# A two-layer graph network on one Trainium2 core: attention matrix and logit row transposed by block loads and VectorE, norm statistics on ScalarE, another order of rounds

## The chip, the cores and the metric

The kernel runs on one core of one Trainium2 chip. A core has TensorE (PE, matrix products; PEld is its weight load), VectorE (DVE), ScalarE (ACT), GpSimd (POOL), and SyncE (SP), whose queue here issues nearly all transfers; 16 DMA engines carry them. The metric is the device time in microseconds of one execution. Before the change the median of three runs is 2782.28 us (2780.95 to 2782.86).

## The reference

There are 64 batches of 256 tokens with 512 features, all in float32, and one 256 x 256 adjacency matrix `adj` of zeros and ones. Two layers follow each other, each with a residual and a norm over the features:

```
# layer 0: masked attention, 8 heads of 64
q, k, v = x @ Wq + bq, x @ Wk + bk, x @ Wv + bv
scores  = q k^T / 8 + (1 - adj) * -1e9
x       = layernorm(x + softmax(scores) v @ Wo + bo)

# layer 1: additive attention
h   = x @ W;   s1 = h . a1;   s2 = h . a2
e   = leaky_relu(s1[i] + s2[j], 0.2) * adj
att = softmax(e)
x   = layernorm(x + elu(att @ h + beta * h))
```

## The kernel before, in words

The batches are taken two at a time ("pairs", 32 of them). Within a pair the stages are named after what TensorE does. `x`: the pair's input is brought in transposed (features on partitions) as `xT`. `q`, `k`, `v`: three projections of both batches together. Then, for each batch `s` of the pair (0 or 1): `scores` (keys by queries, for 8 heads), `sums` (denominators by products with ones), `mix` (attention times v), `o` (output projection, added to the batch's `X`), a norm, `logits` (the row of s2 on all partitions), `attention` (the second attention matrix, transposed), `spread` (X^T times that matrix, giving `yT`), and `u` (the product with `W`). After `u` comes `finish`: elu, residual, norm and the store. The products of `q`, `k`, `v`, `o`, `spread` and `u` are done by seven instead of eight block products (`project`, from line 414); the block sums that this needs are made by POOL (`token_sums` and the sums around line 963). The weights of q and k stream in as seven pieces per pair through six buffers ("piece").

For the second attention, two VectorE products with accumulation (L877) give s1 and s2 per token. TensorE transposes the s2 column, broadcast to 128 columns, into a row on all partitions in PSUM (`pe_row`, L887). VectorE adds s1 (`z`, L896), applies the leaky relu (`e`, L902), POOL multiplies by the mask (L905), VectorE takes the maximum (L907), ScalarE exponentiates with sums (L910), VectorE divides and adds beta to the diagonal (L913, L916). TensorE then transposes the four 128 x 128 blocks of `e` into PSUM (`pe_att`, L923) and ScalarE copies them out as `attT` (L927). Batch 63 ("last") takes a path of its own.

A norm of 128 tokens (`norm`, L553) is bn_stats and bn_aggr on VectorE (L556, L557), the reciprocal root on POOL (L560, L561), minus mean times root on VectorE (L564), and one ScalarE pass over the 512 features with that scale and bias (L566).

The input `xT` is loaded in blocks of 32 x 32 elements (L588: four transfers per batch, one for every group of 32 partitions, pieces of 128 bytes) so that one VectorE instruction, which transposes within blocks of 32 x 32, completes the transpose (L591).

What sets the order: every operation is first recorded with an engine, an estimated cost in ns and its dependences (`Plan.op`). TensorE's order is written by hand: `ROUND` is the cyclic order of stages, and `LATER` says how many rounds after the pair's own number each stage comes. An operation's `claims` name buffers that it takes into use. `Plan.place` then plays the schedule through with the estimated costs, with `LAG` as the time from an operation's end to its effect on another engine (2200 ns for SP), and with the number of buffers in `slots`; the order found is the order in which each engine's instructions are emitted. Each engine, SP's queue among them, then works in that order, and each waits where its next instruction is not ready. The last 60 TensorE operations are free of the written order. A TensorE operation of cost 0 emits nothing; it only fixes from which place of the order its buffers may be claimed.

Of the kernel before, what the change touches and what calls it, by code (L numbers as in the profile page):

```python
# [16 lines left out]
P = 128  # L17
# [4 lines left out]

ROUND = ("sums1", "mix1", "scores0", "v", "o1", "attention0", "u1", "x", "spread0", "sums0", "mix0", "scores1", "q",
         "logits1", "o0", "u0", "attention1", "k", "spread1", "logits0")

LATER = {"x": -2, "q": -1, "k": -1, "v": 0, "scores0": 0, "scores1": 0, "sums0": 0, "sums1": 1, "mix0": 0, "mix1": 1,
         "o0": 0, "o1": 1, "logits0": 0, "logits1": 1, "attention0": 1, "attention1": 1, "spread0": 1, "spread1": 1,
         "u0": 1, "u1": 2}
# [25 lines left out]
class Plan:  # L54
# [9 lines left out]

    LAG = {"PE": 260.0, "DVE": 70.0, "ACT": 70.0, "POOL": 90.0, "SP": 2200.0}
    SWITCH = 250.0
# [161 lines left out]
def gnn_two_layers(ctx: ExitStack, tc: tile.TileContext, x, adj, Wq, bq, Wk, bk, Wv, bv, Wo, bo, W, a, beta, out):  # L228
# [12 lines left out]

    slots = {"xin": 2, "x": 4, "two": 6, "xP": 1, "piece": 6, "full": 4, "half": 18, "xS": 2, "st": 80, "ps": 8, "rows": 4}

# [14 lines left out]
    def sb(tag, shape, name):  # L258
        return Buf(sb_pool, tag, [P] + shape, name)
# [4 lines left out]
    def st(n, name):  # L264
        return sb("st", [n], name)
# [286 lines left out]

    def norm(X, t):  # L553

        bn, mv, rs, nm = st(6, "bn"), st(2, "mv"), st(1, "rs"), st(1, "nmr")
        plan.op("DVE", 690, lambda: nc.vector.bn_stats(bn[A], X[:, t, :]), [(X, (t, 0)), (X, (t, 1))], [bn])  # L556
        plan.op("DVE", 175, lambda: nc.vector.bn_aggr(mv[A], bn[A]), [bn], [mv])  # L557

        def rsqrt():
            nc.gpsimd.tensor_scalar(rs[A], mv[:, 1:2], EPS, None, ALU.add)  # L560
            nc.gpsimd.tensor_tensor(rs[A], rs[A], neg_half, ALU.pow)  # L561

        plan.op("POOL", 800, rsqrt, [mv], [rs])
        plan.op("DVE", 150, lambda: nc.vector.scalar_tensor_tensor(  # L564
            nm[A], mv[:, 0:1], -1.0, rs[A], op0=ALU.mult, op1=ALU.mult), [mv, rs], [nm], mode="two")
        plan.op("ACT", 810, lambda: nc.scalar.activation(  # L566
            X[:, t, :], X[:, t, :], AF.Identity, bias=nm[A], scale=rs[A]),
            [nm, rs], [(X, (t, 0)), (X, (t, 1))])

    def pair(m, at, general=False):  # L570

        def turn(what):

            plan.turn = ((m or 0) + LATER[what], ROUND.index(what))

# [5 lines left out]
        V = sb("two", [2 * NT, D], f"v_{m}")  # L581

        def blocks(s):

            xb = sb("xin", [C, N], f"xin_{m}_{s}")
            rows = x[at].rearrange("o (b j) (c f i) -> o f j c b i", j=32, f=4, i=32)[s]
            for f in range(4):
                plan.op("SP", 700, lambda f=f: nc.sync.dma_start(  # L588
                    xb[f * 32:(f + 1) * 32].rearrange("p c (b i) -> p c b i", i=32), rows[f]), [], [(xb, f)],
                    first=m == 0 and s == 0 and f == 0)  # L590
            plan.op("DVE", 1140, lambda: nc.vector.transpose(  # L591
                xT[A].rearrange("p c (t s n) -> p c t s n", t=NT, s=2)[:, :, :, s, :],
                xb[A].rearrange("p c (t n) -> p c t n", t=NT)), [xb, (xT, "turn")], [(xT, (t, s)) for t in range(NT)])


        turn("x")
        plan.op("PE", 0, lambda: None, [], [(xT, "turn")], claims=[xT])
        for s in range(2):
            blocks(s)

# [33 lines left out]
    def batch(m, s, qT, kT, V, dram, general):  # L634
# [10 lines left out]

        def finish(t, us, u, mode):

            m = sb("half", [D], "m")
            plan.op("ACT", 640, lambda: nc.scalar.activation(m[A], u(), AF.Exp), us, [m])
            plan.op("DVE", 700, lambda: nc.vector.scalar_tensor_tensor(  # L650
                X[:, t, :], u(), 0.0, X[:, t, :], op0=ALU.max, op1=ALU.add), us, tokens(t), mode=mode)
            plan.op("DVE", 700, lambda: nc.vector.scalar_tensor_tensor(
                X[:, t, :], m[A], 1.0, X[:, t, :], op0=ALU.min, op1=ALU.add), [m], tokens(t), mode="two")
            norm(X, t)
            plan.op("SP", 1400, lambda: nc.sync.dma_start(
                dram(out, s)[:, t, :], X[:, t, :]), tokens(t), [])

# [34 lines left out]
        def attention_by_keys():  # L692
# [30 lines left out]
            def denominators():  # L723
                turn("sums")

                acc = ps([N], "ps_den")

                def pe():
                    for i in range(2):
                        for c in range(C):  # L730
                            nc.tensor.matmul(acc[32 * c:32 * c + 32, :], ones[:, 16 - 16 * i:48 - 16 * i],  # L731
                                             both[c][:, i, :], start=i == 0, stop=i == 1)

                plan.op("PE", 1000, pe, both, [acc], mode="sums", claims=[inv])
                plan.op("DVE", 1750, lambda: nc.vector.reciprocal(inv[A], acc[A]), [acc], [inv])
                for i, d in enumerate((acc, inv)):
                    junk = sb("half", [N], "junk")
                    plan.op("ACT", 600, lambda i=i, d=d, junk=junk: nc.scalar.activation(
                        junk[A], d[A], AF.Identity, accum_out=range_sb[:, i, b:b + 1]), [d],
                        [junk, (range_sb, (i, b))])  # L740
                if last:
                    select = sb("half", [H, HD], "select")
                    plan.op("DVE", 690, lambda: nc.vector.tensor_copy(
                        select[A], ident[:, 0:P:P // H].unsqueeze(2).to_broadcast([P, H, HD])), [acc], [select])
                    return [spread_last(select, inv, g) for g in range(2)]
                plan.op("SP", 60, lambda: nc.sync.dma_start(rows[A], inv[0:P:P // H, :]), [inv], [rows])
                for i in range(2):
                    def spread(i=i):
                        r = rows[A]
                        nc.sync.dma_start(everywhere[i * HD:(i + 1) * HD], bass.AP(  # L750
                            tensor=r.tensor, offset=r.offset + i * N, ap=[[0, HD], [2 * N, C], [1, N]]))

                    plan.op("SP", 1500, spread, [rows], [(everywhere, i)])

# [107 lines left out]
        else:  # L862
# [3 lines left out]
            project(left["o"], right_o, False, [], onto, onto)  # L866
        for t in range(NT):
            norm(X, t)
        if b == 0:
            plan.turn = (0, ROUND.index("k"))  # L870
            left["w"] = second_layer_constants()

        sv = [st(2, "s") for t in range(NT)]
        for t in range(NT):
            for i in range(2):
                junk = sb("half", [D], "junk")
                plan.op("DVE", 780, lambda t=t, i=i, junk=junk: nc.vector.scalar_tensor_tensor(  # L877
                    junk[A], X[:, t, :], 1.0, wa_sb[:, i, :], op0=ALU.mult, op1=ALU.mult,
                    accum_out=sv[t][:, i:i + 1]), tokens(t) + [(wa_sb, i)], [junk, (sv[t], i)],
                    mode="two")  # L880


        row = ps([N], "tr_s")

        def pe_row():
            for t in range(NT):
                nc.tensor.transpose(row[:, blk(t)], sv[t][:, 1:2].to_broadcast([P, P]), ident)  # L887

        z, e = sb("half", [NT, N], "z"), sb("half", [NT, N], "e")
        turn("logits")  # L890
        plan.op("PE", 220, pe_row, sv, [row], claims=[z, e])
        nm1, sm1, rc1 = st(NT, "nm1"), st(NT, "sm1"), st(NT, "rc1")
        tra = ps([NT, N], "tr_a")
        attT = sb("half", [NT, N], "attT")
        for t in range(NT):
            plan.op("DVE", 480, lambda t=t: nc.vector.tensor_scalar(  # L896
                z[:, t, :], row[A], sv[t][:, 0:1], None, ALU.add), [row, sv[t]], [(z, t)])

        for ts in ((0, 1), (1, 2)) if last else ((0, 2),):
# [19 lines left out]

            def pe_att(ts=ts):  # L920
                for j in range(NT):
                    for t in range(NT)[ts]:
                        nc.tensor.transpose(tra[:, j, blk(t)], e[:, t, blk(j)], ident)  # L923

            turn("attention")
            plan.op("PE", 215 * k, pe_att, part, [(tra, t) for t in range(NT)[ts]], claims=[attT])
        plan.op("ACT", 590, lambda: nc.scalar.copy(attT[A], tra[A]), [tra], [(attT, i) for i in range(4)])  # L927

        yT = sb("full", [C, N], f"yT_{b}")
        if last:  # L930
# [20 lines left out]
            for t in range(NT):  # L951
                finish(t, [us[t]], lambda t=t: us[t][A], None)
            return
# [37 lines left out]

        for t in range(NT):
            finish(t, [(u, (t, 0)), (u, (t, 1))], lambda t=t: u[:, t, :], "two")

# [65 lines left out]
```

## Time and profile before

| | |
|---|---|
| median of three runs | 2782.28 us |
| the profiled execution | 2782.27 us |
| its span, first to last instruction | 2780.4 us |
| mean granted TensorE clock | 0.995 |
| ACT COPY attT<-tr_a (L927) | 64 times, 586 ns each |
| DVE BATCH_NORM_STATS2 (L556) | 256 times, 681 ns each |
| DVE oT<-oT,inv_all (L776) | 126 times, 894 ns each |
| SP's queue, longest kind of wait (L588 behind DVE yT L478) | 28 times, 832.2 us in all |
| DMA, mean over the span | 94 GB/s; queue q1 34.0% of 16 engines |
| DMA packets | 429313, of them 279448 under 512 B |

How to read it: busy time is the time in which an engine ran at least one instruction. In a group of instructions, the columns are line, engine, operation, out<-in, shapes, count, then busy microseconds and mean ns of one, then the idle time just before them and what ended it. In the chain and in the timeline the columns are start and length in microseconds and what ran. Engines run side by side, and matmuls of TensorE overlap each other in it, so busy times and durations do not add up to the span.

### The profile page before, as it was taken

The numbers are of one execution on the slowest core, as the hardware profiler recorded it, in microseconds if no ns is written. First come the engines' busy times: TensorE is split into PE (matmuls) and PEld (weight loads), VectorE is DVE, ScalarE is ACT, GpSimd is POOL, SyncE is SP. The second block draws the span as 40 slices with busy tenths as digits, with TensorE's granted clock in tenths as the row PEclk, the third lists the DMA queues.
The fourth block names the chain that finished last, engine by engine and source line by source line (L and its number), as shares of the span: only waits on it lengthen the run. The fifth ranks groups of instructions, "written<-read, shape, count | busy, mean of one in ns | idle before, by whom it ended". The sixth has DMA issues, their size and how long they took to land.

```text
span 2780.4 us, 46736 instructions
## 1 busy us (share of the span) xinstructions
PE 2738.3 (98%) x16259; PEld 2312.2 (83%) x16259; DVE 2067.6 (74%) x4190; ACT 1238.7 (45%) x2747; POOL 1759.1 (63%) x2379
## 2 busy tenths in 40 slices
PE   7999999999999999999999999999999999999997
PEld 6788888888888888888888888888888888888875
DVE  6777777787776777777877767777778777677777
ACT  2344444454454444444544544444445445444443
POOL 5666666666666666666666666666666666666664
PEclk9999999999999999999999999999999999999998
DMA  8333332343332433323433324433234332243211
GB/s 220 88 96 107 81 103 68 101 115 96 84 85 80 115 107 80 103 69 100 114 96 84 84 80 114 107 81 102 68 101 115 95 85 85 81 114 92 62 50 36
DMA packets 429313, 260.02 MB, mean 94 GB/s; under 512 B 279448, under 2 KB 360592, under 8 KB 429072
## 3 DMA queue, kind: packets, MB, share of 16 engines
q1 hardware_dynamic: 428944, 256.96, 34.0%
q8 instruction: 132, 2.16, 0.3%
q14 instruction: 109, 0.89, 0.1%
q0 software_dynamic: 128, 0.01, 0.0%
HBM read 220.73 MB, written 36.17 MB: 92 GB/s over the span
## 4 chain that ended last, share of the span: by engine, by line
PE 97%; DVE 2%; issue 0%; SPq 0%; POOL 0%; DMA 0%; ACT 0%; POOLq 0%; DVEq 0%; ACTq 0%
PE ps_chain L433 33%; PE ps_cross L433 22%; PE ps_pair L433 10%; PE ps_sc L708 8%; PE ps_pv L685 8%; PE ps_second L433 6%; PE ps_fourth L433 6%; PE ps_den L731 2%; PE tr_a L923 1%; PE tr_s L887 0%; DVE junk L877 0%; SPq L588 0%; PE ps_y L938 0%; DVE x L650 0%; PE ps_plain L497 0%
## 5 line engine op out<-in xcount | busy, mean ns | idle before, releaser
L719 POOL TENSOR_TENSOR both<-pT 128x256 f32<-128x256 f32 x512 | 369.2, 749 | 46.2 <-ACT pT L717 46.2
L717 ACT ACTIVATE pT<-pT 128x512 f32<-128x512 f32 x512 | 296.5, 625 | 113.6 <-DVE pT L715 113.4
L715 DVE TENSOR_TENSOR pT<-ps_sc,maskT_sb 128x512 f32<-128x512 f32 x512 | 318.1, 679 | 0.2 <-PE ps_sc L708 0.2
L560 POOL TENSOR_SCALAR rs<-mv 128x1 f32<-128x1 f32 x256 | 62.7, 245 | 351.7 <-DVE mv L557 342.8
L708 PE MATMUL ps_sc<-qT,kT 64*128 64x256 f32 x2048 | 238.4, 382 | 0.0
L685 PE MATMUL ps_pv<-pT,v 128*64 128x256 f32 x2048 | 235.1, 382 | 0.0
L708 PEld LDWEIGHTS ps_sc<-qT,kT 64*128 64x128 f32 x2048 | 192.8, 187 | 44.4 <-issue 24.2
L685 PEld LDWEIGHTS ps_pv<-pT,v 128*64 128x64 f32 x2048 | 141.3, 137 | 91.0 <-issue 25.9
L566 ACT ACTIVATE x<-x,nmr,rs 128x512 f32<-128x512 f32 x256 | 204.0, 811 | 8.1 <-DVE nmr L564 6.5
L877 DVE SCALAR_TENSOR_TENSOR junk<-x,wa_sb 128x512 f32<-128x512 f32 x256 | 195.4, 800 | 0.0
L404 POOL TENSOR_TENSOR yS<-yT 128x256 f32<-128x256 f32 x126 | 103.4, 820 | 144.1 <-DVE yT L478 139.1
L910 ACT ACTIVATE e<-e,nm 128x256 f32<-128x256 f32 x128 | 64.7, 506 | 255.5 <-DVE nm L907 255.5
L561 POOL TENSOR_TENSOR rs<-rs,neg_half 128x1 f32<-128x1 f32 x256 | 155.3, 607 | 21.3
L669 POOL TENSOR_TENSOR x<-x,res_sb 128x512 f32<-128x512 f32 x128 | 161.7, 1284 | 7.8 <-DMA x<-in_x_dram 6.4
L556 DVE BATCH_NORM_STATS2 bn<-x 128x6 f32<-128x512 f32 x256 | 164.2, 681 | 2.2
L963 POOL TENSOR_TENSOR X_sums<-x 128x256 f32<-128x256 f32 x126 | 107.1, 850 | 66.4 <-ACT x L566 66.4
L927 ACT COPY attT<-tr_a 128x512 f32<-128x512 f32 x64 | 37.5, 586 | 244.3 <-PE tr_a L923 243.9
L404 POOL TENSOR_TENSOR xS<-xT 128x512 f32<-128x512 f32 x64 | 81.7, 1277 | 92.6 <-PE ps_chain L433 83.0
L404 POOL TENSOR_TENSOR oS<-oT 128x256 f32<-128x256 f32 x126 | 98.1, 779 | 65.9 <-DVE oT L776 59.7
L905 POOL TENSOR_TENSOR e<-e,adj_sb 128x512 f32<-128x512 f32 (+1 forms) x65 | 82.1, 1263 | 85.5 <-DVE e L902 84.1
L771 ACT COPY oT<-ps_pv 128x512 f32<-128x512 f32 x128 | 75.1, 586 | 131.8 <-PE ps_pv L685 129.6
L433 PE MATMUL ps_chain<-sw_sb,yS 128*128 128x256 f32 x504 | 129.3, 379 | 0.0
(230 smaller groups left out, 7260.1 us busy)
## 6 DMA issues: line engine op xcount, KB each, us to landing
xin<-in_x_dram SPq DMA_DIRECT2D x256, 128.0 KB
x<-in_x_dram SPq DMA_DIRECT2D x64, 512.0 KB
out_dram<-x SPq DMA_DIRECT2D x128, 256.0 KB
inv_all<-rows SPq DMA_DIRECT2D x126, 256.0 KB
wq_sums<-wq_sums SPq DMA_DIRECT2D x124, 256.0 KB
wk_sums<-wk_sums SPq DMA_DIRECT2D x124, 256.0 KB
wq_sums<-in_L_gnn_Wq_dram SPq DMA_DIRECT2D x93, 256.0 KB
wk_sums<-in_L_gnn_Wk_dram SPq DMA_DIRECT2D x93, 256.0 KB
```

What stands on the lines that cost most here:

```text
L404: plan.op("POOL", 180 + 545 * width // P, lambda: nc.gpsimd.tensor_tensor(dst(), p(), m(), ALU.subtract), reads, writes)
L433: nc.tensor.matmul(dst[:, f, :], lhs, rhs, start=start and f == 0 and c == 0, stop=c == inner - 1, skip_group_check=True)
L556: plan.op("DVE", 690, lambda: nc.vector.bn_stats(bn[A], X[:, t, :]), [(X, (t, 0)), (X, (t, 1))], [bn])
L561: nc.gpsimd.tensor_tensor(rs[A], rs[A], neg_half, ALU.pow)
L566: plan.op("ACT", 810, lambda: nc.scalar.activation(X[:, t, :], X[:, t, :], AF.Identity, bias=nm[A], scale=rs[A]), [nm, rs], [(X, (t, 0)), ...
L669: plan.op("POOL", 1270, lambda t=t: nc.gpsimd.tensor_tensor(X[:, t, :], X[:, t, :], res_sb[A], ALU.add), [res_sb], tokens(t))
L685: nc.tensor.matmul(acc[r * HD:(r + 1) * HD, i, :], V[:, 2 * k + s, h * HD:(h + 1) * HD], pT[h][:, k, :], start=k == 0, stop=k == NT - 1)
L708: nc.tensor.matmul(acc[j][:, k, :], kT[r:r + HD, c, key_blk(k)], own(qT, r, c), start=True, stop=True)
L715: plan.op("DVE", 690, lambda h=h, i=i: nc.vector.tensor_add(pT[h][A], acc[i][A], maskT_sb[A]), [acc[i], maskT_sb], [pT[h]])
L717: plan.op("ACT", 620, lambda h=h: nc.scalar.activation(pT[h][A], pT[h][A], AF.Exp, scale=1.0 / HD ** 0.5), [pT[h]], [pT[h]])
L719: plan.op("POOL", 725, lambda h=h, i=i: nc.gpsimd.tensor_tensor(both[c][:, i, :], pT[h][:, 0, :], pT[h][:, 1, :], ALU.add), [pT[h]], [(bot ...
L877: plan.op("DVE", 780, lambda t=t, i=i, junk=junk: nc.vector.scalar_tensor_tensor(junk[A], X[:, t, :], 1.0, wa_sb[:, i, :], op0=ALU.mult, o ...
```

## The change

The second attention of batches 0 to 62 is no longer transposed by TensorE. `e` is written to a DRAM buffer (`square`), loaded back in blocks of 32 x 32 elements by four transfers (`att_b`), and turned inside the blocks by one VectorE transpose. The row of logits is made likewise: s1 and s2 of a batch lie in a buffer of 2 x 32 columns (`sv`, one of four that are cleared once), VectorE transposes it in blocks, a transfer writes the s2 parts to a DRAM line of 256 numbers, and a second one reads the line onto all partitions. Batch 63 keeps TensorE for both.

The norm is computed for both tiles of a batch together: ScalarE sums the features (Identity with accumulation) and, with minus the mean as bias, the squares; VectorE makes the mean from the sum; POOL makes the root and minus mean times root; ScalarE's normalizing pass stays. `finish` takes both tiles together (one after the other for batch 63).

The input of pair 0 is loaded by plain transfers and transposed by TensorE with copies by ScalarE; the other pairs keep the block loads. `ROUND` has a new order, `spread1` comes one round later, and `LAG` of SP is 4200 instead of 2200 ns; the costs that the planner is told for some transfers change too.

```diff
-ROUND = ("sums1", "mix1", "scores0", "v", "o1", "attention0", "u1", "x", "spread0", "sums0", "mix0", "scores1", "q",
-         "logits1", "o0", "u0", "attention1", "k", "spread1", "logits0")
+ROUND = ("sums1", "mix1", "scores0", "spread1", "v", "u1", "attention0", "sums0", "mix0", "scores1", "o1", "x",
+         "logits1", "q", "spread0", "o0", "attention1", "u0", "k", "logits0")
...
-         "o0": 0, "o1": 1, "logits0": 0, "logits1": 1, "attention0": 1, "attention1": 1, "spread0": 1, "spread1": 1,
+         "o0": 0, "o1": 1, "logits0": 0, "logits1": 1, "attention0": 1, "attention1": 1, "spread0": 1, "spread1": 2,
...
-    LAG = {"PE": 260.0, "DVE": 70.0, "ACT": 70.0, "POOL": 90.0, "SP": 2200.0}
+    LAG = {"PE": 260.0, "DVE": 70.0, "ACT": 70.0, "POOL": 90.0, "SP": 4200.0}
...
-        plan.op("DVE", 690, lambda: nc.vector.bn_stats(bn[A], X[:, t, :]), [(X, (t, 0)), (X, (t, 1))], [bn])
-        plan.op("DVE", 175, lambda: nc.vector.bn_aggr(mv[A], bn[A]), [bn], [mv])
...
+            plan.op("ACT", 700, lambda: nc.scalar.activation(
+                junk[A], X[:, t, :], func, bias=mean[:, i:i + 1] if bias else 0.0, accum_out=to[:, i:i + 1]),
+                [(X, (t, 0)), (X, (t, 1))] + ([mean] if bias else []), [junk, (to, i)])
+        for i, t in enumerate(ts):
+            total(i, t, AF.Identity, sums, False)
+        plan.op("DVE", 110, lambda: nc.vector.tensor_scalar(mean[A], sums[A], -1.0 / D, None, ALU.mult), [sums], [mean])
+        for i, t in enumerate(ts):
+            total(i, t, AF.Square, sq, True)
...
+            nc.gpsimd.tensor_scalar(rs[A], sq[A], 1.0 / D, EPS, ALU.mult, ALU.add)
+            nc.gpsimd.tensor_tensor(rs[A], rs[A], neg_half[A].to_broadcast([P, n]), ALU.pow)
+            nc.gpsimd.tensor_tensor(nm[A], mean[A], rs[A], ALU.mult)
...
+            rows = sb("xin", [NT, D], f"xin_{m}_{s}")
+            for t in range(NT):
+                plan.op("SP", 700, lambda t=t: nc.sync.dma_start(rows[:, t, :], dram(x, s)[:, t, :]), [], [(rows, t)],
+                        first=s == 0 and t == 0)
...
+                        nc.tensor.transpose(tr[:, c, :], rows[:, t, blk(c)], ident)
...
-        plan.op("PE", 220, pe_row, sv, [row], claims=[z, e])
+            line, row = Buf(dram_pool, "line", [N], "line"), sb("half", [N], "row")
+            plan.op("PE", 0, lambda: None, [], [(row, "turn")], claims=[z, e, row])
+            svT = sb("svT", [NT, 32], "svT")
+            plan.op("DVE", 180, lambda: nc.vector.transpose(svT[A], sv[A]), s2 + [(row, "turn")], [svT])
+            plan.op("SP", 500, lambda: nc.sync.dma_start(
+                line[A].rearrange("(t g j) -> g t j", t=NT, j=32), svT[0:P:32]), [svT], [line])
+            plan.op("SP", 500, lambda: nc.sync.dma_start(row[A], row_on_all(line[A], 0, N)), [line], [row])
...
-            plan.op("PE", 215 * k, pe_att, part, [(tra, t) for t in range(NT)[ts]], claims=[attT])
-        plan.op("ACT", 590, lambda: nc.scalar.copy(attT[A], tra[A]), [tra], [(attT, i) for i in range(4)])
+            square, att_b = Buf(dram_pool, "square", [N, N], "square"), sb("half", [NT, N], "att_b")
+            plan.op("PE", 0, lambda: None, [], [(att_b, "turn")], claims=[attT, att_b])
+            plan.op("SP", 500, lambda: nc.sync.dma_start(
+                square[A].rearrange("(t p) j -> p t j", p=P), e[A]), [e], [square])
+            for f in range(4):
+                plan.op("SP", 720, lambda f=f: nc.sync.dma_start(
+                    att_b[f * 32:(f + 1) * 32].rearrange("p k (b i) -> p k b i", i=32),
+                    square[A].rearrange("(b j) (k f i) -> f j k b i", j=32, f=4, i=32)[f]),
+                    [square, (att_b, "turn")], [(att_b, f)])
+            plan.op("DVE", 660, lambda: nc.vector.transpose(attT[A], att_b[A]), [att_b], [(attT, i) for i in range(4)])
```

## The prediction

> **What bounds the kernel now.** I read the page's busy times, then its chain, then the waits of TensorE, then one stretch of the chain in order of time.
>
> ```profile
> span 2780.4 us, 46736 instructions
> ...
> PE 2738.3 (98%) x16259; PEld 2312.2 (83%) x16259; DVE 2067.6 (74%) x4190; ACT 1238.7 (45%) x2747; POOL 1759.1 (63%) x2379
> ...
> PE 97%; DVE 2%; issue 0%; SPq 0%; POOL 0%; DMA 0%; ACT 0%; POOLq 0%; DVEq 0%; ACTq 0%
> ```
>
> TensorE has work for 98% of the span, and the chain that ended last is 97% TensorE. So a microsecond off the TensorE stream counts in full, and a microsecond off VectorE counts only if TensorE waited for it. It hardly did:
>
> ```profile
> PE ps_chain L433 <- DVE xT L591: 12.5, 1, 12.5
> PE ps_chain L433 <- DVE pT L715: 6.4, 1, 6.4
> PE ps_pair L433 <- DVE nmr L564: 4.0, 1, 4.0
> PE tr_a L923 <- POOL rs L560: 3.6, 1, 3.6
> ```
>
> Each of these waits (total, times, longest) happened once: 12.5 us at the start, 6.4 us at 71.5 us, the others after 2695 us. From about 96 to 2677 us TensorE never waits; in the chain one point of the round recurs at 1031.12 and at 1116.08 us, 84.96 us per pair of batches. The transposes lie in that stream (start, length, what):
>
> ```profile
> 1035.55 0.45 PE ps_chain L433 x4
> 1035.99 0.22 PE tr_s L887 x2
> 1036.21 1.00 PE ps_den L731 x16
> ...
> 1061.93 0.86 PE ps_chain L433 x4
> 1062.80 0.44 PE tr_a L923 x4
> 1063.23 0.87 PE ps_chain L433 x4
> ```
>
> Four attention transposes move the stream on by 0.44 us, the two of the row of logits by 0.22 us.
>
> **Transposes off TensorE.** The groups of instructions invite a larger number:
>
> ```profile
> L923 PE MATMUL tr_a<-ident,e 128*128 128x128 f32 x256 | 38.6, 273 | 4.4 <-POOL rs L560 3.6 <-DVE nmr L564 0.7
> ...
> L887 PE MATMUL tr_s<-ident,s 128*128 128x128 f32 x128 | 24.7, 274 | 1.2 <-DVE pT L715 0.6 <-DVE junk L877 0.6
> ```
>
> One record lasts 273 ns, but they overlap each other and their neighbours: start to start it is 109 ns. The Trainium skill (TensorE: Matmul & The Clock Gate, PE-mode transpose) puts a transpose at about 275 ns inside a kernel. By that, six per batch over the 63 batches that change give 378 x 0.275 = 104 us; by the busy sums 63 us; by the stream 63 x (0.44 + 0.22) = 41.6 us. I take the last, since the next matmul's start is what the end depends on. Mode switches (sums, columns, rows, plain) stay six per round in the new order, so nothing there. Round: 84.96 - 1.32 = 83.64 us.
>
> **What takes their place.** Per batch: one small VectorE transpose, two transfers for the row (line out, row broadcast 128 KB), one 256 KB write of the attention, four block loads of 64 KB in pieces of 128 B, one VectorE transpose of 128x512. The nearest rows are the x blocks, loaded and transposed in just this way:
>
> ```profile
> L591 DVE STREAM_TRANSPOSE xT<-xin 128x1024 f32<-128x1024 f32 x64 | 78.8, 1232 | 2.5 <-DMA xin<-in_x_dram 2.2 <-issue 0.3
> ```
>
> and, for SP's queue in order of time (start, length of issue, what):
>
> ```profile
> 1072.33 2.92 SPq L588 DMA_DIRECT2D xin<-in_x_dram  x4
> 1075.79 0.62 SPq L746 DMA_DIRECT2D rows<-inv  x1
> 1077.85 1.30 SPq L750 DMA_DIRECT2D inv_all<-rows  x2
> ```
>
> VectorE: half of 1232 ns, 0.62 us, plus about 0.15 us: 0.77 x 63 = 49 us. Issue on SP: about 0.73 us per block load and 0.3 to 0.6 us per other: 4.5 us a batch, 9 us a round, on a queue that has 10 to 30 us holes. Transfers: 512 KB of x blocks kept the 16 DMA engines busy from about 1074.0 to 1077.3 us, 3.3 us; half is 1.7 us, the write at the 305 GB/s of the best slice 0.9, the row 0.45: 3 us x 63 = 190 us, from 34% to about 41% of the DMA engines. A rule speaks against this: the skill (DMA: Bandwidth & Descriptors, Rules for kernel authors) wants no transpose by a plain DMA with a rearranged pattern, 19 times slower. By it the four loads take 19 x 0.86 = 16 us (0.86: 256 KB at that 305 GB/s), by the row 1.7 us; the row decides, since it is the same 32x32 pattern, where the turning inside a block is left to VectorE.
>
> So the chain of a batch grows by latency. Rows to inv_all shows a hop: 8 KB issued at 1075.79 released the next issue at 1077.85, 2.1 us. Added hops: line 2.1, row about 3 (4 if x blocks are ahead), square about 2.5, blocks 2.9 of issue and 2.5 to land: some 13 us, less about 2 us for what they replace. Unloaded, from the last product of `o` to the start of `spread` I add up about 30 us: norm 6.5, logit sums 3.3, row 5, z to e 7 (with its reads and waits), attention hops 8, sums on POOL 2.5 (4 x 0.62). What hides it is the new order. With the stream's own lengths (sums, mix, scores 8.4; v, q, k 12.05; o, u 6.03; spread 3.09), `o0` to `spread0` has 74 us (55 before) and `o1` to `spread1`, now a round later, 48 us (55 before). So at least 18 us are left for queueing in the tighter one. If that cover is gone, each missing microsecond is paid 31 times.
>
> **Waits that are new, and who stands behind them.** SP waits for `e` before the write of the attention; behind it is the seventh piece of the k weights, whose buffer comes free 1.7 us into `k` and which is needed 10.4 us into it. By my sums `e` is ready about at the start of `k`, so some 9 us are left. VectorE waits for the row before `z` and for the blocks before the transpose; behind them are additions that free PSUM banks for `o` and `u`. The planner allows 4.2 us plus issue per hop, about 2 us more than the hop in the trace, so these come late in VectorE's queue rather than early. The shortest distance made new: `spread0` to `u0` is now only `o0`, 6.03 us (some 27 us before); `u0`'s second product needs two VectorE additions (0.42 each) and two POOL sums (about 0.8): 2.6 us, so 4 us for queueing. From both sides: no stall, or up to 1 us a round (31 us). I take none, as TensorE does not wait in any round of before.
>
> **Norms on ScalarE.** VectorE loses bn_stats 164.2, aggregate 36.2, nmr 56.6 = 257 us and gains about 20 (130 means near the 152 ns of a 128x2 reciprocal). POOL: 256 pairs of 245 + 607 ns become about 130 triples, the third op between 0.25 and 0.6 us: 218 to about 150 us. ScalarE gains 512 passes. Its nearest rows:
>
> ```profile
> L738 ACT ACTIVATE junk<-inv 128x256 f32<-128x256 f32 x64 | 26.9, 420 | 3.2 <-DVE inv L735 3.2
> ...
> L910 ACT ACTIVATE e<-e,nm 128x256 f32<-128x256 f32 x128 | 64.7, 506 | 255.5 <-DVE nm L907 255.5
> ...
> L910 ACT ACTIVATION_READ_ACCUMULATOR e<-e,nm 128x1 f32 x128 | 24.1, 188 | 0.0
> ```
>
> 256 more columns cost 213 ns (625 for the 512-wide exp against about 412 for 256): 0.82 us for the sum, 0.91 for the square with its bias, both with the read. 256 x 1.73 = 443 us, less 37 for the attT copies: 1645 us, 60%. VectorE ends near 1860 us (68%). Neither bounds, so this is worth nothing in the rounds. At the end it costs: in the last batch bn to the normalizing pass took 2.09 us (2772.66 to 2774.75); the new chain is about 3.4 us. Two norms are exposed: +3 us. Batch 62, now with four hops, must fit there too; its chain from `o0` to the end sums to some 75 us beside about 85 us for batch 63, so I add nothing (0 to +10 in the range). More of the work is left over for this end (about 64 us of matmuls after the last scores, 54 before), which can fill the holes: down to -8.
>
> **The start.** Pair 0 is loaded by 4 plain transfers ahead of the weights instead of 8 block loads (0.74 to 8.2 us of issue) and turned by TensorE (16 x 0.11, slower while the clock is low) and ScalarE (4 x 0.6). First q product at about 7.5 us, when the first half of Wq has landed, instead of 12.46: -5. The 6.4 us stall at 71.5 us came from seven 1.74 us products of VectorE ahead of the additions; five stand there now: -1 to -6. I take -6 for both.
>
> **Sum.** 2782.27 (the profiled execution, 1.9 us beyond its span; the median of the three runs is 2782.28) - 41.6 - 6 + 3 = 2737.7, so 2738 us.
>
> **Rivals.**
> 1. Small stalls in each round, at `u0` after `spread0` or by a late piece of weights: 0.5 us x 31 = 16, giving about 2754 (2746 to 2776). For it: the 4 us distance, and queues already 68% busy. Against: not one such wait before. 0.15.
> 2. Slower: the write of the attention blocks SP past the 9 us, the seventh k piece comes late, and TensorE waits every round. For it: one in-order queue, seven more issues a batch. It decides from 1.6 us a round (44.6 + 5.6 over 31); at 3 us late beyond the slack, 93 - 44.6 gives about 2830. Against: a hop of 2.1 us where the plan has over 4. 0.07.
> 3. The busy sums are right (63 us), or the end fills up well: about 2714. Against: the stream's own starts. 0.05.
> 4. Nothing moves, as new waits give back all: 2782. 0.02. That the transposes remain on TensorE is excluded: its stream has them only for pair 0's x and the last batch.
> My forecast: 0.71.
>
> The range, 2722 to 2768, takes in the bounds of start and end and most of rival 1. About 0.2% (5.6 us) is what a measurement can tell here. Faster: 0.71 + 0.15 + 0.05 = 0.91; same 0.02; slower 0.07.
>
> **What would show it.** Right: a round of 83.6 us with no TensorE waits between 100 and 2600 us, PE busy near 2690, ACT near 60%, DVE near 68%, the first q product before 9 us. Wrong: a wait of TensorE that occurs about 31 times (behind yS it is rival 1, behind a weight piece rival 2), or a round shorter than 83.4 us.

## The result, and the profile after

After the change the median of four runs is 2736.07 us (2734.59 to 2736.42), against 2782.20 us (2780.95 to 2782.86, four runs): ratio 0.9834 [0.9817, 0.9851]. The prediction was 2738.0 us, range 2722 to 2768. The profiled execution took 2734.59 us, its span is 2732.8 us, 47.6 us less than before.

The page's busy times, answering to the first fence of the prediction:

```profile
span 2732.8 us, 47289 instructions
...
PE 2698.5 (99%) x15897; PEld 2268.1 (83%) x15897; DVE 1960.9 (72%) x3676; ACT 1549.5 (57%) x3712; POOL 1728.6 (63%) x2261
```

TensorE still has work for 99% of the span; ScalarE has 311 us more work, VectorE only 107 us less. The waits of TensorE (total, times, longest), the first two, and the one that stands where the 6.4 us stall of before was:

```profile
PE tr_x L608 <- DMA xin<-in_x_dram: 4.1, 2, 3.7
PE ps_inv L802 <- DVE select L783: 2.8, 1, 2.8
...
PE ps_b L520 <- DVE pT L750: 0.5, 1, 0.5
```

None occurs once a round: `tr_x` is the start, `ps_inv` is in batch 63, and the last is at 62.2 us, before the first round. Between 88 and 2659 us no wait of TensorE is longer than 0.05 us. So the rounds are pure TensorE stream, as before. Their length is read from two starts of the same product, one round apart, in the timeline; between them lies the way of the attention of one batch:

```profile
1005.75 1.07 PE L766 MATMUL ps_den<-both,ones 128*32 128x256 f32 x16
...
1077.38 0.38 SPq L983 DMA_DIRECT2D square<-e  x1
...
1081.41 2.59 SPq L986 DMA_DIRECT2D att_b<-square  x4
...
1086.72 0.70 DVE L990 STREAM_TRANSPOSE attT<-att_b 128x512 f32<-128x512 f32 x1
...
1089.39 1.07 PE L766 MATMUL ps_den<-both,ones 128*32 128x256 f32 x16
...
1097.65 0.71 PE L433 MATMUL ps_chain<-attT,x 128*128 128x128 f32 x4
```

The round is 83.64 us, to the hundredth the 84.96 - 1.32 of the prediction. `e` leaves 0.17 us after `k` begins (1077.21 us), and the turning of `attT` starts 10.9 us before `spread1` takes it. Over the 29 rounds between the same denominators of pair 2 and pair 31 the difference is 38.56 us (2464.19 against 2425.63), 1.33 a round.

Where the 47.6 us lie: the first output projection starts at 75.21 instead of 85.96 us, after equal work: 10.75. The transposes give 63 x 0.66 = 41.6. What remains is 47.6 - 10.75 - 41.6 = -4.75, a loss. It is found by subtraction; the traces place it at the end: there 14.7 us instead of 10.5 pass from TensorE's last product to the end of the span, and TensorE's waits in the last batches add up to 12.6 us instead of 11.4. (Some 1.2 us of short waits that before has at 133 to 146 us are gone too; the prediction had counted none there.)

### The profile page after: what moved, and what is told of

Read it like the earlier page. It is cut to its first block, busy times and chain, and to the rows that moved or that the text cites. A ratio compares the mean times of both kernels' runs of the same rounds, so it can differ in the third digit from the quotient of the medians.

```text
span 2732.8 us, 47289 instructions
## 1 busy us (share of the span) xinstructions
PE 2698.5 (99%) x15897; PEld 2268.1 (83%) x15897; DVE 1960.9 (72%) x3676; ACT 1549.5 (57%) x3712; POOL 1728.6 (63%) x2261
## 3 DMA queue, kind: packets, MB, share of 16 engines
q1 hardware_dynamic: 581220, 298.34, 41.7%
## 5 line engine op out<-in xcount | busy, mean ns | idle before, releaser
L917 DVE SCALAR_TENSOR_TENSOR junk<-x,wa_sb 128x512 f32<-128x512 f32 x256 | 207.8, 837 | 110.3 <-ACT x L581 109.2
L469 ACT COPY u<-ps_chain 128x256 f32<-128x256 f32 x126 | 47.0, 373 | 319.2 <-PE ps_chain L433 318.7
L1026 POOL TENSOR_TENSOR X_sums<-x 128x256 f32<-128x256 f32 x126 | 150.9, 1207 | 99.5 <-ACT x L581 99.5
L564 ACT ACTIVATE junk<-x,mean 128x512 f32<-128x512 f32 x256 | 182.2, 714 | 6.4 <-DVE mean L570 6.4
L564 ACT ACTIVATE junk<-x 128x512 f32<-128x512 f32 x256 | 159.4, 625 | 36.5 <-DVE x L894 33.7
L704 POOL TENSOR_TENSOR x<-x,res_sb 128x512 f32<-128x512 f32 x128 | 176.3, 1380 | 0.0
L575 POOL TENSOR_SCALAR rs<-sq 128x2 f32<-128x2 f32 x130 | 34.9, 269 | 194.3 <-ACT junk L564 189.0
L404 POOL TENSOR_TENSOR oS<-oT 128x256 f32<-128x256 f32 x126 | 92.1, 731 | 84.2 <-DVE mean L570 52.5
L816 DVE TENSOR_TENSOR oT<-oT,inv_all 128x512 f32<-128x512 f32 x126 | 134.7, 1107 | 0.0
L433 PE MATMUL ps_chain<-so_sb,oS 128*128 128x256 f32 x504 | 129.3, 379 | 0.0
L778 DVE RECIPROCAL inv<-ps_den 128x256 f32<-128x256 f32 x64 | 112.5, 1757 | 17.1 <-PE ps_den L766 8.7
```

Source lines behind the costliest of these rows:

```text
L404: plan.op("POOL", 180 + 545 * width // P, lambda: nc.gpsimd.tensor_tensor(dst(), p(), m(), ALU.subtract), reads, writes)
L433: nc.tensor.matmul(dst[:, f, :], lhs, rhs, start=start and f == 0 and c == 0, stop=c == inner - 1, skip_group_check=True)
L564: plan.op("ACT", 700, lambda: nc.scalar.activation(junk[A], X[:, t, :], func, bias=mean[:, i:i + 1] if bias else 0.0, accum_out=to[:, i:i ...
L704: plan.op("POOL", 1270, lambda t=t: nc.gpsimd.tensor_tensor(X[:, t, :], X[:, t, :], res_sb[A], ALU.add), [res_sb], tokens(t))
L1026: plan.op("POOL", ns, lambda: nc.gpsimd.tensor_tensor(dst(), p(), m(), op), reads, writes)
```

## The experiments

Twelve kernels were run, all but one of them the kernel after with something put back or added. All compute the whole reference. Each ratio is to the kernel before on the same chip (medians 2780.92, 2781.80 and 2781.88 us in the three groups).

### One part of the change undone

**row_on_pe** and **att_on_pe**: in the kernel after, the row of logits, or the attention, goes back to TensorE (the one condition that keeps it there for batch 63 is made true for all).

```diff
-        if last:
+        if True:
```

> The changed kernel, with only the row of logits given back to TensorE in all batches. Stream theory (what leaves TensorE's stream counts, start to start): 63 x 0.22 = 13.9 us slower than the changed kernel, 2750 us, a round of 84.08 us. Busy-sum theory (a transpose is worth its share of busy time, 24.7 us for 128): 63 x 0.386 = 24 us slower, 2760 us. Order theory (the new order of rounds brought the gain, the transposes' place is of no account): 2736 us.

Measured 3097.08 us, 1.1138 [1.112, 1.1157]: far above every figure expected. The wait of TensorE says why:

```profile
PE tr_s L933 <- DVE junk L917: 256.8, 63, 8.1
```

In the new order `logits1` follows `o1` directly (`x` emits nothing on TensorE there). TensorE arrives before the logit sums exist and waits in every round, once for each of the two tiles. After such a pair of waits it is also slow: at 1569.57 us, behind 7.63 and 0.59 us, the next two groups of eight products took 3.4 and 2.5 us from start to start instead of 1.73 each, 2.5 us more. The granted clock is 0.58 in these groups, 1.00 in the 7 us behind them, and 0.946 over the whole run.

> The changed kernel, with only the attention matrix given back to TensorE in all batches (copies out of PSUM by ScalarE as before). Stream theory: 63 x 0.44 = 27.7 us slower than the changed kernel, 2764 us, a round of 84.52 us. Busy-sum theory (38.6 us for 256 transposes): 63 x 0.603 = 38 us slower, 2774 us. Order theory: 2736 us.

Measured 2898.85 us, 1.0425 [1.0408, 1.0443]:

```profile
PE tr_a L976 <- DVE e L966: 78.6, 30, 3.7
```

Again a place that is too early: `attention1` stands ahead of `u0`, and in the kernel after `e` is ready only at the start of `k`, one `u0` (6.03 us) later. Neither kernel measures the price of the transposes; both show that the new order can't be had with them where they are. So each was given a place that fits.

**att_fit**: attention on TensorE, `attention1` moved behind `k`.

```diff
-         "logits1", "q", "spread0", "o0", "attention1", "u0", "k", "logits0")
+         "logits1", "q", "spread0", "o0", "u0", "k", "attention1", "logits0")
```

> The changed kernel, with the attention matrix transposed by TensorE again, and only attention1 moved from ahead of u0 to behind k, where e is ready by the changed kernel's trace. Stream theory, mended: 27.7 us slower than the changed kernel, 2764 us, a round of 84.52 us. If the long way by transfers was needed for another reason: far above, as the 2899 us without the move.

Measured 2771.47 us, 0.9963 [0.9949, 0.9977], 35.4 us above after. The round is 85.24 us, 1.60 more: twice 0.53 us from a `tr_a` to the product behind it, and a wait that is once per round:

```profile
PE ps_pair L433 <- DVE yT L478: 17.0, 31, 1.0
```

Over 29 rounds that is 46.8 us in the trace; the end gives 9.9 back (98.3 instead of 108.2 us from the last `sums0` of the rounds to the end of the span). That batches 60 to 62 have no transfers in their way there is the probable reason; it isn't shown. So four attention transposes cost TensorE 0.53 us a batch at this place, not 4 x 273 ns.

**row_fit**: row on TensorE, `logits1` moved behind `q`, `logits0` behind `spread1` of the next round.

```diff
-ROUND = ("sums1", "mix1", "scores0", "spread1", "v", "u1", "attention0", "sums0", "mix0", "scores1", "o1", "x",
-         "logits1", "q", "spread0", "o0", "attention1", "u0", "k", "logits0")
+ROUND = ("sums1", "mix1", "scores0", "spread1", "logits0", "v", "u1", "attention0", "sums0", "mix0", "scores1", "o1",
+         "x", "q", "logits1", "spread0", "o0", "attention1", "u0", "k")
...
-         "o0": 0, "o1": 1, "logits0": 0, "logits1": 1, "attention0": 1, "attention1": 1, "spread0": 1, "spread1": 2,
+         "o0": 0, "o1": 1, "logits0": 1, "logits1": 1, "attention0": 1, "attention1": 1, "spread0": 1, "spread1": 2,
...
-        if last:
+        if True:
```

> The changed kernel, with the row of logits on TensorE again, but its two places in the order of rounds moved to where its numbers are ready by the changed kernel's trace: logits1 after q, logits0 after spread1 of the next round. Stream theory, mended (only start to start counts, as long as TensorE finds its data ready): 13.9 us slower than the changed kernel, 2750 us, a round of 84.08 us, no wait of TensorE at these transposes. If the row on TensorE is slow for a reason of its own (its PSUM bank, the planner's new order of VectorE): far above, as the 3097 us of the run without the move.

Measured 2939.98 us, 1.056 [1.054, 1.0579]. The waits at `tr_s` are gone from the rounds, but another has come at `spread1`:

```profile
PE ps_chain L433 <- ACT yT L469: 123.9, 29, 5.7
```

It is the wait that the next kernel explains. The price of the row by itself was not found.

**norm_on_vector**: bn_stats and bn_aggr on VectorE again (the old `norm` for each tile), all else as after.

```diff
-            total(i, t, AF.Identity, sums, False)
...
-            total(i, t, AF.Square, sq, True)
+        plan.op("DVE", 690, lambda: nc.vector.bn_stats(bn[A], X[:, t, :]), [(X, (t, 0)), (X, (t, 1))], [bn])
+        plan.op("DVE", 175, lambda: nc.vector.bn_aggr(mv[A], bn[A]), [bn], [mv])
```

> The changed kernel, with the norm statistics back on VectorE (bn_stats, bn_aggr, two POOL steps and the VectorE product, tile by tile). Stream theory: the rounds stay at 83.64 us, and the end gets shorter by the two exposed norms, about 3 us: 2733 us. Relief theory (the 257 us taken off VectorE are what lets the transposes go there): TensorE waits in every round, 0.5 us or more, 2750 us and above.

Measured 2970.45 us, 1.0683 [1.0665, 1.07]: slower than before by far more than the change gains. The round is 92.1 us. One stall in the timeline, all engines in order of time:

```profile
1551.37 1.68 DVE L940 TENSOR_SCALAR z<-row,s 128x256 f32<-128x256 f32 x2
1553.08 1.09 DVE L946 SCALAR_TENSOR_TENSOR e<-z 128x512 f32<-128x512 f32 x1
1554.10 2.35 DVE L810 TENSOR_TENSOR oT<-oT,inv_all 128x512 f32<-128x512 f32 x2
...
1556.52 0.37 ACT L469 COPY yT<-ps_chain 128x256 f32<-128x256 f32 x1 [4.41 <-DVE oT L810]
...
1557.04 1.19 PE L433 MATMUL ps_chain<-att_sums,X_sums 128*128 128x128 f32 x4 [6.37 <-ACT yT L469]
```

`spread1`'s fourth product needs the PSUM bank that ScalarE's copy into `yT` empties. The copy waits for VectorE's product of `oT` with the inverse denominators `inv_all`, and in VectorE's queue that product stands behind eight additions of scores, `z` and `e`. Why a copy into `yT` depends on it can be read from the kernel: `yT`, `oT`, `inv_all`, `u` and `X_sums` take turns in four buffers of one kind ("full"). `oT` is still to be read by `o1`, so the buffer that comes free with this product must be that of `inv_all`, which it is the last to read. No run isolates this. In the kernel after no `yT` copy waits for `oT`: there the additions of `yT` (1099.36 us) come first and the product later (1106.96). VectorE has 184 us more work here than in after, but is busy for 72% of the span in both. lag_2200 below has the same stall with no more VectorE work than after (1921.5 us), so a wrong order in its queue is enough for it. row_fit shows the same pair (ACT `yT` behind DVE `oT`, 67.1 us, 29 times).

### One part done alone

**norm_alone**: the kernel before with only the norms on ScalarE, both tiles together.

```diff
-        for t in range(NT):
-            norm(X, t)
+        for ts in ([0], [1]) if last else ([0, 1],):
+            norm(X, ts)
```

> The kernel before, with only the norm statistics moved to ScalarE (and both tiles finished together). Stream theory: the rounds stay at 84.96 us and the end gets longer by about 3 us: 2785 us. Relief theory: some us faster than before, 2775 us or less.

Measured 2807.38 us, 1.0097 [1.008, 1.0113]: slower than either theory had it. The round is 85.90 us, 0.94 longer. ScalarE's two normalizing passes (1.52 us, 1555.93 us) now stand ahead of the `yT` copies; TensorE waits for those (8.8 us, 30 times, 0.29 us a round), and with the slower products behind the wait it loses 0.53 us a round there. The rest are smaller delays at the other `spread` (0.3 us) and behind `scores` (0.16 us). The start is as before, with its waits of 12.5 and 6.4 us.

**old_order**: the kernel after with the `ROUND` and `LATER` of before (`LAG` stays 4200).

> The changed kernel with the order of rounds and the round of spread1 of the kernel before (4200 ns per transfer in the planner kept). There o to spread has 55 us in both batches, and o1 comes before the attention stages. Stream theory as predicted (30 us of unloaded chain fit into 55): 2736 to 2745 us, a round near 83.6 us. Rival (the new order is what makes the transposes' longer way fit): TensorE waits in every round, at spread or behind VectorE, 1 us a round or more, above 2770 us.

Measured 3122.55 us, 1.1225 [1.1206, 1.1243]. TensorE's wait and one case of it:

```profile
PE ps_chain L433 <- DVE attT L990: 228.6, 60, 7.3
```

```profile
1557.68 2.62 SPq L986 DMA_DIRECT2D att_b<-square  x4
...
1568.31 0.69 DVE L917 SCALAR_TENSOR_TENSOR junk<-x,wa_sb 128x512 f32<-128x512 f32 x1 [1.21 <-ACT x L581]
...
1569.27 0.70 DVE L990 STREAM_TRANSPOSE attT<-att_b 128x512 f32<-128x512 f32 x1
...
1570.11 0.68 PE L433 MATMUL ps_chain<-attT,x 128*128 128x128 f32 x4 [1.82 <-DVE attT L990]
```

The blocks are issued by 1560.3 us and land 2.3 us later (median of the page for this kernel), but VectorE turns them only at 1569.27 us: they stand behind a logit product that itself waits for ScalarE. In 29 of the 60 cases VectorE waits for the blocks themselves (105.8 us). From the row's issue (1539.25) to that of `square` (1555.54) it takes 16.3 us here, 10.3 in the kernel after (1067.09 to 1077.38). So the long way doesn't fit the old order as it is scheduled with this allowance. Whether it would with another was not tried.

### How much room the new order leaves

**hop_1** and **hop_3**: in the kernel after the attention takes one, or three, more DRAM buffers of 256 KB on its way (`range(1)`, `range(3)`); the planner is not told.

```diff
-            plan.op("SP", 500, lambda: nc.sync.dma_start(
-                square[A].rearrange("(t p) j -> p t j", p=P), e[A]), [e], [square])
+            def out_and_on():
+                src = e[A]
+                for i in range(1):
+                    hop = dram_pool.pool.tile([N, N], F32, tag=f"hop_{i}", name=f"hop_{i}", bufs=4)
+                    to = hop.rearrange("(t p) j -> p t j", p=P)
+                    nc.sync.dma_start(to, src)
+                    src = to
+                nc.sync.dma_start(square[A].rearrange("(t p) j -> p t j", p=P), src)
+
+            plan.op("SP", 500, out_and_on, [e], [square])
```

> The changed kernel with the attention matrix taken through one more DRAM buffer on its way (a second 256 KB transfer behind the first, some 2.5 us in which SP's queue stands still, not known to the planner, so the order of every engine stays). My 9 us of slack behind SP and 8 us ahead of spread1: no change, 2736 to 2740 us. Rival 2 (the queue is at its limit): about 2.5 us in every round, 2810 us.

Measured 2734.75 us, 0.9833 [0.9817, 0.9849], as after. VectorE now waits for the blocks 22 times, 7.7 us in all; TensorE doesn't notice.

> After, with three more DRAM buffers in the attention's way (256 KB each, write and plain read back between them; the planner is not told), everything computed. One extra buffer cost nothing; three add about 7 to 8 us to the way of attT, all on SP's queue behind which the k weights and the x blocks stand. Theory (some 9 us are left from e to the need for the seventh k piece and for attT): just at the edge, 2736 to 2760, with TensorE waits of at most 1 us a round. Rival (the slack is small, 2 to 4 us): a wait of 4 us or more in each round, 2860 or more. If nothing at all happens (under 2740), the distance is larger than I worked out.

Measured 2909.79 us, 1.0457 [1.0441, 1.0473], 5.6 us a round: the rival's side. A part comes by the way I had in mind: the weight pieces of `k` stand behind the hops on SP's queue, and TensorE waits for them for 34.6 us (18 times). A larger part comes by another way, for which these lines stand, a group of TensorE's waits and a case of it in the timeline:

```profile
PE ps_pair L433 <- DVE pT L750: 47.2, 30, 2.8
```

```profile
1548.24 2.62 SPq L994 DMA_DIRECT2D att_b<-square  x4
...
1552.54 0.71 DVE L998 STREAM_TRANSPOSE attT<-att_b 128x512 f32<-128x512 f32 x1 [4.62 <-DMA att_b<-square]
...
1553.88 1.42 PE L433 MATMUL ps_pair<-wo_sb,oT 128*128 128x256 f32 x4 [2.85 <-DVE pT L750]
```

TensorE doesn't use this `attT` before 1572.34 us. What is late is what stands behind it in VectorE's queue: additions of scores, which free the PSUM bank that a product of `o` needs. VectorE waits for blocks in 62 batches, 291.8 us in all.

**lag_2200**: the kernel after, planned with 2200 instead of 4200 ns behind a transfer.

> After, with the planner told 2200 ns instead of 4200 ns from a transfer's end to its effect; the written order of TensorE is the same. Theory (the transposes behind a transfer then come too early in VectorE's queue and hold the additions up, which the stage order cannot make good): waits in each round, at least 1 us, 2765 or more. Rival (the written order alone has room enough, the allowance is worth nothing): 2736 within 4 us.

Measured 3032.36 us, 1.089 [1.0873, 1.0907]. TensorE waits for the `yT` copy 26 times, 113.4 us, the largest of several kinds of waits (the next two, behind VectorE's `x`, are 35.4 and 18.0 us). A case of it in the timeline:

```profile
1500.12 4.88 DVE L750 TENSOR_TENSOR pT<-ps_sc,maskT_sb 128x512 f32<-128x512 f32 x8 [2.24 <-PE ps_sc L743]
...
1506.36 1.87 DVE L816 TENSOR_TENSOR oT<-oT,inv_all 128x512 f32<-128x512 f32 x2 [1.36 <-DMA inv_all<-rows]
...
1508.30 0.37 ACT L469 COPY yT<-ps_chain 128x256 f32<-128x256 f32 x1 [2.64 <-DVE oT L816]
```

It is the stall of norm_on_vector. The plan has put the product of `oT` ahead of the `yT` additions, since it believes `inv_all` to be there. In the chip it takes 8.4 us from the issue of `rows` (1497.97) to that product. The allowance does not make the transfers faster; it keeps what depends on them from standing at the head of VectorE's queue too early.

### The start and the end

**blocks_start**: pair 0 loaded in blocks and turned by VectorE, as before.

```diff
-        if m == 0:
-            for s in range(2):
-                turned(s)
-        else:
+        if True:
```

> After, with pair 0's input loaded in blocks and turned by VectorE as before the change; everything else as after. In the two traces q of pair 1 starts 8.4 us earlier in after and q1 ends 10.8 us earlier. Theory A (the start's gain is the plain loading: first product earlier, and no cold clock): this kernel is 9 to 11 us slower than after, about 2746. Theory B (half of it comes from the order of VectorE's products and the norms, which stay here): 4 to 6 us slower, about 2741. No difference would mean that the start is bound by the weights' arrival.

Measured 2737.97 us, 0.9845 [0.9831, 0.9858], 1.9 us above after, which the medians alone can't tell from nothing; the two traces show 2.0. Either way it is less than either theory. The timeline of its TensorE, first product and first output projection:

```profile
11.89 3.78 PE L433 MATMUL ps_chain<-xT,wq_sb 128*128 128x256 f32 x8 [11.89 <-DVE xT L622]
...
77.24 1.03 PE L433 MATMUL ps_chain<-wo_sb,oT 128*128 128x256 f32 x4
```

The first product starts 4 us later than in after (7.91), but only 2.0 us are left at the output projection (77.24 against 75.21): in after the third group of products waits 2.04 us for POOL's sums, and is slow behind that. So plain loading gives 2.0 of the start's 10.75 us. Of the other 8.7, 0.6 are there before the stall (the first product starts at 11.89 us here and at 12.46 in before). 8.1 are the stall that is gone: 6.37 us of waiting and 1.84 + 0.50 of slow products behind it (3.57 and 2.23 from start to start instead of 1.73), less the 0.54 us of waiting that is left.

What takes it away can be seen in VectorE's queue. Ahead of the additions of scores that TensorE waits for stand products that sum the weights (L538). First before, then after, each with what TensorE does then:

```profile
64.11 1.75 DVE L538 SCALAR_TENSOR_TENSOR junk<-w_sb,a 128x512 f32<-128x512 f32 x1
...
65.27 1.71 POOL L669 TENSOR_TENSOR x<-x,res_sb 128x512 f32<-128x512 f32 x1
...
71.53 3.78 PE L433 MATMUL ps_chain<-xT,wq_sums 128*128 128x256 f32 x8 [6.37 <-DVE pT L715]
```

```profile
60.20 0.68 DVE L538 SCALAR_TENSOR_TENSOR junk<-w_sb,a 128x512 f32<-128x512 f32 x1
...
62.16 1.12 PE L520 MATMUL ps_b<-bv_wo,ones 128*128 128x512 f32 x2 [0.54 <-DVE pT L750]
...
62.91 2.11 POOL L754 TENSOR_TENSOR both<-pT 128x256 f32<-128x256 f32 x3 [3.79 <-ACT pT L752]
```

In before there are seven of them, and six take 1.74 us each while POOL is at work beside them. In after there are five: 1.34 and 1.74 us beside POOL, then three of 0.68 us while POOL stands idle (59.11 to 62.91 us). old_order, which has everything but the new order, still waits 2.85 us at this place, with POOL busy and the last four products at 1.74 to 1.75 us. norm_alone has the whole stall, so norms on ScalarE alone don't remove it; blocks_start has it no more, so plain loading isn't needed for that. The new order is; whether it would do alone was not run.

**end_norms**: bn_stats norms in batches 62 and 63 only.

```diff
+        if b is None or b < 62:
+            return norm_scalar(X, ts)
+        for t in ts:
+            norm_tile(X, t)
```

> After, with bn_stats norms on VectorE again in batches 62 and 63 only, ScalarE's norms in all others; everything computed. I had put +3 us on the two exposed norms of the end. Theory: that is given back, 2733 (about 3 us faster than after), and this is then the fastest version. Rival (batch 62's norms on VectorE put its queue behind, as in all batches before): no gain or slower, 2736 to 2742.

Measured 2728.80 us (2727.49 to 2730.33, five runs), 0.9809 [0.9795, 0.9822]: faster than both kernels, by 7.3 us of medians against after (4.3 in the two profiled spans), more than the 3 us expected. The last norm in after and in end_norms, from the statistics to the normalizing passes:

```profile
2722.31 0.63 ACT L564 ACTIVATE junk<-x 128x512 f32<-128x512 f32 x1 [0.76 <-DVE x L687]
...
2726.77 1.52 ACT L581 ACTIVATE x<-x,nmr,rs 128x512 f32<-128x512 f32 x2 [1.37 <-POOL nmr L577]
```

```profile
2718.97 1.28 DVE L588 BATCH_NORM_STATS2 bn<-x 128x6 f32<-128x512 f32 x2
...
2721.51 2.36 ACT L598 ACTIVATE x<-x,nmr,rs 128x512 f32<-128x512 f32 x3 [0.15 <-DVE nmr L596]
```

It takes 5.98 us by ScalarE (to 2728.29) and 4.90 by VectorE (to 2723.87; the first of the three passes in the last line belongs to batch 63).

## Why the prediction was right, and where it was not

- **The stream, 41.6 us: right.** The round is exactly the one worked out. Rival 3 (busy sums of 63 us) falls: TensorE's busy time fell by 39.8 us, and att_fit pays 0.53 us for four transposes. That is also against the 275 ns apiece of the Trainium skill (TensorE: Matmul & The Clock Gate, PE-mode transpose; given there for one kernel, behind a measurement in bf16), by which four would take 1.1 us: that is the length of one record, not its share of a full stream.
- **What replaces them is hidden: right, with the wrong reason.** DMA came to 41.7% (forecast 41%). But I measured the room as the time from `o` to `spread`, 18 us beyond my unloaded sum of 30, and in `k` as 9 us. The runs show less: one hop passes, three cost 5.6 us a round, while the attention in the shown case of hop_3 is still 19 us early. The room is the time by which the planner has put the VectorE transpose behind the blocks' arrival. In after it starts 7.0 us (median of 63, the least is 3.0) behind the issue of the last block, and a block lands some 2.3 us behind its issue, which leaves about 4.7 us. (Of the 16 us that the prediction had weighed for the four loads nothing shows.) In hop_1 the 7.0 us are 4.4, in hop_3 they are 2.5: nothing is left. The prediction's sentence that VectorE's additions for PSUM banks stand behind its waits was the right mechanism, and its sum should have been made there. (The terms of the unloaded sum, called 30 us, add up to 32.) old_order shows the same from the other side: 55 us were not enough where 48 are.
- **Norms on ScalarE "worth nothing in the rounds": failed.** I argued from shares of busy time (neither engine bounds). norm_on_vector loses 234 us without them, norm_alone loses 26 us with them in the old order. Both come from the place of single instructions in two queues, on engines busy for 41 to 72% of the time. As far as these two runs show, the norms on ScalarE are a condition of the schedule, not a gain of their own.
- **Rival 1 (small stalls each round) and rival 2 (late weights on SP's queue): not in after.** Neither `u0` after `spread0` nor a weight piece makes TensorE wait. But how near they were I had not seen: a planner's allowance 2 us shorter turns the gain into a loss of 9%.
- **The start: -6 forecast, -10.75 measured.** Plain loading was put at -5 and gave 2.0; the stall at 71.5 us was put at -1 to -6 and gave 8.1, as it vanished nearly whole (0.54 left) and took the slow products behind it along. The prediction counted rightly five products of VectorE where seven had stood, but priced each at 1.74 us; three of them take 0.68 with POOL idle.
- **The end: +3 forecast, +4.75 measured.** The loss is known by subtraction only. The new chain of a norm was sized nearly right: 3.5 us for one tile (batch 63, 2711.49 to 2714.98) against the 3.4 of the prediction, 4.5 for the two of batch 62. What was left out is that the last product is now of batch 62, whose `finish` has more behind it: 14.7 us from TensorE's last product to the end, 10.5 before. end_norms gives back 4.3 us of it in the spans: its last norm is 1.1 us shorter, the way from TensorE's last product to that norm is 1.0 us shorter, and TensorE's last product ends 2.4 us earlier (2715.7 against 2718.1), for which no reason was found.
- **Busy times.** VectorE 1961 us instead of 1860. The prediction's own terms add up to 1880, as 20 us for the means had been left out of the sum. Of the other 81, 27 us are the products of `oT` with `inv_all`, which got longer (below); the rest is spread over many groups. ScalarE 1549.5 instead of 1645: the accumulator reads (190 ns) overlap the passes, 625 and 714 ns, where I had added them. Neither makes TensorE wait in a round.

Start and end erred by -4.75 and +1.75 us, which left the sum at 2738 by some luck: with their own sizes it would have been 2735.

What stays open: what the new order is worth without the other parts was not run, nor the old order with a shorter allowance, nor a kernel that only gives `yT` and `inv_all` separate buffers, which would test the recurring stall by itself. The price of the row's transposes was measured only together with that of the attention's. The gain at the start was not divided further between the order of VectorE's queue and what POOL does beside it.

## What to carry to other kernels

Price what leaves the bounding engine by start-to-start times in its stream, and then ask of everything that replaces it not whether its engine has time, but what stands behind it in that engine's queue, and whose PSUM bank or buffer that frees. Where a hand-written order, a planner's allowance and the division of work over engines were fitted together, undoing one of them measures the misfit, not the part; give a removed part a place that fits before reading its price. At the end of a kernel, where nothing hides latency, keep the version with the shortest chain even if the rounds want another.

## What the runs showed of the hardware

A wait of TensorE costs more than its length. These are stretches right behind a wait, from before (6.4 us), row_on_pe (8.2) and att_on_pe (2.5), each with the granted clock as the third number from the end; the second line of before is the stretch that follows on the first:

```profile
71.53:77.33 5.80, 5.80 (x16) 4.75 (x17) 5.28 (x8) 3.78 (x7) 3.79 (x6) 0.61 0.13 30
77.33:85.96 8.63, 8.63 (x41) 7.60 (x40) 4.72 (x5) 4.08 (x9) 5.71 (x9) 1.00 0.85 227
...
1570.88:1576.79 5.91, 5.91 (x18) 4.79 (x17) 3.42 (x7) 0.84 (x2) 3.69 (x5) 0.58 0.28 62
...
1851.94:1855.62 3.68, 3.68 (x11) 2.98 (x12) 0.42 (x2) 2.60 (x8) 1.76 (x4) 0.54 0.02 4
```

In them the products took 2.3, 2.5 and 1.7 us longer than elsewhere. The loss grows far less than the wait: behind 2.5 us of waiting 1.7 are lost, behind 8.2 us 2.5. att_on_pe has 27 such stretches for its 30 waits.

VectorE operations with two SBUF operands vary with what runs beside them:

```profile
L816 DVE TENSOR_TENSOR oT<-oT,inv_all 128x512 f32<-128x512 f32 x126 | 134.7, 1107 | 0.0
...
L1026 POOL TENSOR_TENSOR X_sums<-x 128x256 f32<-128x256 f32 x126 | 150.9, 1207 | 99.5 <-ACT x L581 99.5
```

Before, these were 894 and 850 ns. One such VectorE product lasts from 649 to 1760 ns in after. Over the whole trace of after, the 61 of the 126 with POOL idle beside them (at most 5% of their time busy) took 649 to 684 ns; the 33 that lie wholly beside POOL's work (95% or more) took 678 to 1709, on average 1320. The products of the start show the same, 1.74 us beside POOL and 0.68 without it. POOL is slower then too: the two products at 1106.96 us took 3.02 us together while POOL ran two operations of 128x512, one of them 1.72 instead of 1.27 us. That the two engines slow each other is read from these; no run changes POOL's work alone.
